# Turning the token rows of an expert block: two of three blocks by VectorE after a load in shares, the rest by TensorE

## The chip, the cores and the metric

The kernel runs on one core of a Trainium2 chip. The metric is the device time of one launch in microseconds (us); the profile is of one execution on the same core. All data are float32.

## What is computed

The input is 8 batches of 512 tokens with 256 features. Four layers follow one another, each with a layer norm ahead of it and a residual sum behind it: a state-space scan, a mixture of experts, causal attention with 16 heads, and the same mixture of experts once more. The change is in the mixtures of experts:

```python
x = hidden_states.reshape(-1, D)                    # 4096 tokens, D = 256
topk_idx, tw = _route(x, router_w, bias)            # 4 of 16 experts each
combine = (one_hot(topk_idx, E) * tw[..., None]).sum(1)
h = jnp.einsum('td,edf->etf', x, gate_w)            # F = 256
u = jnp.einsum('td,edf->etf', x, up_w)
y = jnp.einsum('etf,efd->etd', silu(h) * u, down_w)
routed = jnp.einsum('etd,te->td', y, combine)
sh = silu(x @ sh_gate_w) * (x @ sh_up_w) @ sh_down_w
return routed + sh
```

## The kernel before

The program runs in four stretches: the scan together with the first routing and the shared experts; the first routed stage; attention together with the second routing and shared experts; the second routed stage. Only the routed stages and what feeds them are touched.

**Sorted rows.** While a batch is routed, GpSimd scatters each token's row, once per chosen expert, into a DRAM buffer `xg[i]` that is sorted by expert. A row has 272 numbers: 256 normed features, 4 gains, 4 expert numbers and 8 copies of the token's number. A routed stage then goes through `xg[i]` in blocks of 128 rows, each of one expert; 136 blocks (`LIKELY`, L43) are always run.

**One block**, in `routed` (L823):

- `load` (L850): SyncE issues one DMA of 128 rows of 1088 B (L860) into a buffer `rows`. From block 2 on these come from a ring of nine (`KB`, L57), so the load of block n waits until the accumulation of block n - 9 has read its buffer.
- `fetch` (L863): ScalarE copies the expert's gate weights, VectorE its up weights, out of `w_all`, which holds all experts, into tiles with fixed addresses (L875). The place in `w_all` is a register value; `values` (L830) reads such values for four blocks at a time, the weights' places for TensorE, ScalarE and VectorE and the rows' places for SyncE.
- `turn` (L878): TensorE transposes the two halves of 128 features with the identity (`pt`, L882), and ScalarE copies the result back beside the rows (L883).
- `up` (L885): 8 matmuls, which the profile shows as 16 (L893), give gate and up products in one PSUM tile `ph` of a pool of four; ScalarE takes the sigmoid of the gate half (L901), VectorE multiplies twice (L902, L903) and works out each row's gain (L906, L914).
- `down` (L917): 2 matmuls, shown as 4 (L921); ScalarE scales the rows by their gain (L929); GpSimd adds them with an indirect DMA to the tokens' rows of a DRAM sum, `parts[i][n % 2]` (L930), so that even and odd blocks have a sum each.

**Order.** `run` (L940) writes the order out by hand: load n + 2, fetch n + 1, up n, turn n + 1, down n - 2. Engines run on their own and in order, so SyncE's loads run ahead as far as buffers come free. A scheduler may move an instruction within its engine's order unless it is pinned. Beside the blocks, at set block numbers, GpSimd's queue also carries other DMAs: in the first routed stage those that fetch a finished batch for attention (`prepared`, L1212, after block 64 and at the end), in the second those that fetch and store the sums of five finished batches (`early`, L1443, from blocks 64, 76, 88, 110 and 127). After the last accumulation the remaining batches are summed and stored.

PSUM pools of a routed stage are made by `banks_of(big=4, misc=2, y=2)` (L1412, L1420).

Of the kernel before, what the change touches and what calls it, by code (L numbers as in the profile page):

```python
# [11 lines left out]
AF = mybir.ActivationFunctionType  # L12
ALU = mybir.AluOpType
AX = mybir.AxisListType

P = 128
SQ = 32
QUAD = P // SQ
B, T, D = 8, 512, 256
NT = T // P  # L20
KD = D // P
# [37 lines left out]
PACE = 2  # L59
SENT = 4  # L60
HELD = 6


SUMMED = {0: DONE[0], 1: 76, 2: 88, 3: 110, 4: 127}
# [12 lines left out]
def tile_hybrid_block(  # L77
# [31 lines left out]
    def bank(shape, name: str, kind: str = "one"):  # L109
        kind = instead.get(kind, kind)  # L110
        return stage[kind].tile(shape, FP, tag=kind, name=name)

    def banks_of(**many):
        pools = ExitStack()
        for kind, bufs in many.items():
            stage[kind] = pools.enter_context(
                tc.tile_pool(name=f"ps_{kind}", bufs=bufs, space=bass.MemoryType.PSUM)
            )
        return pools
# [96 lines left out]
    def load_expert(e: int):  # L216
        at = e * WEXP
        gu = w_all[:, at : at + 2 * KD * F].rearrange("p (s k f) -> p s k f", k=KD, s=2)
        nc.sync.dma_start(out=gu[:, 0], in_=gate_w[e].rearrange("(k p) f -> p k f", p=P))
        nc.sync.dma_start(out=gu[:, 1], in_=up_w[e].rearrange("(k p) f -> p k f", p=P))  # L220
        nc.sync.dma_start(
            out=w_all[:, at + 2 * KD * F : at + WEXP].rearrange("p (k d) -> p k d", k=KF),
            in_=down_w[e].rearrange("(k p) d -> p k d", p=P),
        )
# [244 lines left out]
    class Scan:  # L469
# [7 lines left out]
        def load(self, b: int):  # L477
            if b + 1 < B and b > 0:
                with tc.issue_after(load_x(b + 1).ins):
                    for load in later[b - 1 :: shares]:  # L480
                        load()
# [341 lines left out]
    def routed(i: int, table, beside):  # L823

        weight_at, row_at, expert, many, _ = table
        ACT, DVE = mybir.EngineType.Activation, mybir.EngineType.DVE
        PE, SP = mybir.EngineType.PE, mybir.EngineType.SP
        held = {}

        def values(n: int):  # L830

            many = min(4, (LIKELY if n < LIKELY else NBLK) - n)
            _, w = nc.values_load_multi_w_load_instructions(
                weight_at[:, n : n + many],
                engines=[PE, ACT, DVE],
                min_val=0,
                max_val=(E - 1) * WEXP,
                skip_runtime_bounds_check_because="a count of at most E - 1 experts, times WEXP",
            )
            _, r = nc.values_load_multi_w_load_instructions(  # L840
                row_at[:, n : n + many],
                engines=[SP],
                min_val=0,
                max_val=NROW - BLK,
                skip_runtime_bounds_check_because="the blocks table stays within the sorted rows",
            )
            for j in range(many):
                held[n + j] = [w[j], r[j]]

        def load(n: int):  # L850
            if n not in held:
                values(n)
            if n < 2:


                rows = work.tile([P, NT, ROW], FP, tag="rows", name=f"rows_{i}_{n}")
                rows = rows.rearrange("p t c -> p (t c)")[:, 0 : 4 * D]
            else:
                rows = work.tile([P, 4 * D], FP, tag="kb4", name=f"rows_{i}_{n}", bufs=KB)
            nc.sync.dma_start(out=rows[:, 0:ROW], in_=xg[i][bass.ds(held[n][1], BLK), :])  # L860
            held[n].append(rows)

        def fetch(n: int):  # L863


            if n == 0:

                both = xpool.tile([P, NT, D], FP, tag="x", name=f"both_{i}").rearrange("p t d -> p (t d)")
            for half, (copy, name) in enumerate(((nc.scalar.copy, "gate"), (nc.vector.tensor_copy, "up"))):
                if n == 0:  # L870
                    here = both[:, half * KD * F : (half + 1) * KD * F]
                    copy = nc.vector.tensor_copy
                else:
                    here = work.tile([P, KD * F], FP, tag="col", name=f"{name}_{i}_{n}", bufs=COLS)
                copy(here, w_all[:, bass.ds(held[n][0] + half * KD * F, KD * F)])  # L875
                held[n].append(here)

        def turn(n: int):  # L878
            rows = held[n][2]
            pt = bank([P, KD, P], f"pt_{i}_{n}", "misc")  # L880
            for k in range(KD):
                nc.tensor.transpose(pt[:, k, :], rows[:, k * P : (k + 1) * P], ident)  # L882
            nc.scalar.copy(rows[:, ROW : ROW + D], pt.rearrange("p k q -> p (k q)"))  # L883

        def up(n: int):  # L885
            _, _, rows, *both = held[n]


            ph = bank([P, 2, KF * P], f"ph_{i}_{n}", "big")
            for s in range(2):  # L890
                for f in range(KF):
                    for k in range(KD):
                        nc.tensor.matmul(  # L893
                            ph[:, s, f * P : (f + 1) * P],
                            lhsT=both[s][:, k * F + f * P : k * F + (f + 1) * P],
                            rhs=rows[:, ROW + k * P : ROW + (k + 1) * P],
                            start=(k == 0),
                            stop=(k == KD - 1),
                        )
            act = rows[:, ROW + D : ROW + D + F]  # L900
            nc.scalar.activation(act, ph[:, 0, :], AF.Sigmoid)  # L901
            nc.vector.tensor_mul(act, ph[:, 0, :], act)  # L902
            nc.vector.tensor_mul(act, ph[:, 1, :], act)  # L903

            gain = small.tile([P, TK + 1], FP, tag="gain", name=f"gain_{i}_{n}", bufs=4)
            nc.vector.scalar_tensor_tensor(  # L906
                gain[:, 0:TK],
                rows[:, D + TK : D + 2 * TK],
                expert[:, n : n + 1],
                rows[:, D : D + TK],  # L910
                ALU.is_equal,
                ALU.mult,
            )
            nc.vector.tensor_reduce(gain[:, TK : TK + 1], gain[:, 0:TK], AX.X, ALU.add)  # L914
            held[n][3:] = [act, gain]

        def down(n: int):  # L917
            w, _, rows, act, gain = held.pop(n)
            py = bank([P, D], f"pyr_{i}_{n}", "y")
            for f in range(KF):  # L920
                nc.tensor.matmul(  # L921
                    py,
                    lhsT=act[:, f * P : (f + 1) * P],
                    rhs=w_all[:, bass.ds(w + 2 * KD * F + f * D, D)],
                    start=(f == 0),
                    stop=(f == KF - 1),
                )

            nc.scalar.mul(rows[:, 0:D], py, gain[:, TK : TK + 1])  # L929
            nc.gpsimd.indirect_dma_start(  # L930
                out=parts[i][n % 2],
                out_offset=bass.IndirectOffsetOnAxis(
                    ap=rows[:, D + 2 * TK : D + 2 * TK + 1].bitcast(U32), axis=0
                ),
                in_=rows[:, 0:D],
                in_offset=None,
                compute_op=ALU.add,
            )

        def run(first: int, last: int):  # L940
            load(first)
            load(first + 1)
            fetch(first)
            turn(first)
            for n in range(first, last + 2):
                if n + 2 < last:
                    load(n + 2)
                if n + 1 < last:
                    fetch(n + 1)
                if n < last:  # L950
                    up(n)
                if n + 1 < last:
                    turn(n + 1)
                if n - 2 >= first:
                    down(n - 2)
                    for work_beside in beside.get(n - 1, ()):
                        work_beside()


        _, (needed,) = nc.values_load_multi_w_load_instructions(  # L960
            many, min_val=0, max_val=NBLK, skip_runtime_bounds_check_because="a count of blocks"
        )
        with tc.If(needed > LIKELY):
            run(LIKELY, NBLK)
        run(0, LIKELY)
# [443 lines left out]
        table = stretch(Scan())  # L1409
        wqkv_sb, wo_sb = load_attention_weights()  # L1410

    with banks_of(big=4, misc=2, y=2):  # L1412
        instead["one"] = "misc"
        routed(0, table, {**prepared(0), **prepared(1)})
        del instead["one"]
# [1 line left out]
    with banks_of(one=4, pair=2):  # L1417
        table = stretch(Attention())

    with banks_of(big=4, misc=2, y=2):  # L1420

        beside = (nc.gpsimd, nc.gpsimd)

# [123 lines left out]
```

## Time and profile before

| what | before |
|---|---|
| median of 4 runs, lowest to highest | 1727.91 us, 1725.86 to 1729.31 |
| the profiled execution's own time, and its span | 1728.91 us, 1727.2 us |
| mean granted TensorE clock | 0.982 |
| busy: TensorE, its weight loads, VectorE | 95%, 70%, 66% of the span |
| busy: ScalarE, GpSimd | 44%, 45% |
| first routed stage: first load to last accumulation | 339.8 to 752.2 us |
| second routed stage: first load to last accumulation | 1281.1 to 1708.2 us |
| load of rows (SyncE), issue to landing | 2.6 us median, 272 of them |
| accumulation (GpSimd), issue to landing | 4.0 us median, 272 of them |

Busy shares are means over stretches of different kinds, so they have to be read stretch by stretch. Matmuls are pipelined: the time that one takes from the next is seen from start to start, not in its length. A "releaser" behind an arrow is the one whose event came last before an engine went on, as the profile infers it.

### The profile page before, as it was taken

What the parts mean: (1) busy time and instruction counts of PE and PEld (TensorE: products, weight loads), DVE (VectorE), ACT (ScalarE), POOL (GpSimd) and SP (SyncE); (2) the same over time, 40 slices, a digit from 0 to 9 for tenths busy, and PEclk for the clock granted to TensorE, in tenths of its full rate; (3) what the DMA queues carried; (4) which work ended last, traced back from release to release, by engine and by line L of the source; (5) the groups of instructions that cost most, each with busy time, mean ns of one, the idle gap of its engine ahead of it and who ended that gap; (6) DMA issues with size and microseconds to landing.
All of it is one profiled execution on the core that took longest, in us unless ns stands there. A gap on an engine that the chain in (4) does not pass through costs nothing. (4 is left out here: it accounts for less than half of the span.)

```text
span 1727.2 us, 32460 instructions
## 1 busy us (share of the span) xinstructions
PE 1634.7 (95%) x10448; PEld 1207.9 (70%) x10448; DVE 1131.9 (66%) x3503; ACT 767.6 (44%) x1684; POOL 771.4 (45%) x675
## 2 busy tenths in 40 slices
PE   6899998999999999999999999999999999999992
PEld 3566655589999999954445445444459999998992
DVE  7888877545555655567886687777735755555552
ACT  3223232155555555555444444444225555555551
POOL 3355555535555655530042242233434555555553
PEclk9999999999999999999999999999999999999996
DMA  5454333445555656531012211122544656666666
GB/s 161 138 183 157 135 107 114 161 90 96 96 97 106 108 96 96 101 74 38 25 65 69 70 62 60 64 83 85 178 142 83 96 95 97 114 132 125 115 123 165
DMA packets 149277, 181.36 MB, mean 105 GB/s; under 512 B 16144, under 2 KB 135984, under 8 KB 149104
## 3 DMA queue, kind: packets, MB, share of 16 engines
q0 software_dynamic: 54720, 82.57, 25.9%
q1 hardware_dynamic: 92576, 92.71, 18.0%
q10 hardware_dynamic: 1808, 3.93, 0.6%
q8 instruction: 88, 1.44, 0.3%
q14 instruction: 85, 0.70, 0.1%
HBM read 81.62 MB, written 97.53 MB: 104 GB/s over the span
## 5 line engine op out<-in xcount | busy, mean ns | idle before, releaser
L930 POOL DMA_INDIRECT part<-rows x272 | 425.2, 1563 | 345.5 <-ACT rows L929 241.7
L723 POOL DMA_INDIRECT xg<-sorted_m,slots_m x256 | 259.3, 1013 | 319.9 <-ACT slots_m L720 81.8
L893 PEld LDWEIGHTS ph<-rows,gate 128*128 128x128 f32 x2160 | 282.6, 192 | 15.6 <-ACT rows L883 1.6
L893 PE MATMUL ph<-rows,gate 128*128 128x128 f32 x2160 | 286.0, 276 | 0.6 <-ACT rows L883 0.6
L893 PE MATMUL ph<-rows,up 128*128 128x128 f32 x2160 | 285.9, 276 | 0.0
L921 PE MATMUL pyr<-w_all,rows 128*128 x1088 | 280.0, 380 | 0.4 <-DVE rstd_l L431 0.4
L893 PEld LDWEIGHTS ph<-rows,up 128*128 128x128 f32 x2160 | 263.5, 193 | 0.0
L901 ACT ACTIVATE rows<-ph 128x256 f32<-128x256 f32 x272 | 104.2, 383 | 330.0 <-PE ph L893 330.0
L902 DVE TENSOR_TENSOR rows<-ph,rows 128x256 f32<-128x256 f32 x272 | 115.2, 424 | 190.0 <-ACT rows L901 189.1
L921 PEld LDWEIGHTS pyr<-w_all,rows 128*128 128x128 f32 x1088 | 185.8, 191 | 14.7 <-ACT rows L929 0.8
L875 ACT COPY gate<-w_all 128x512 f32 x270 | 168.7, 626 | 14.3 <-PE ph L893 2.4
L1131 ACT ACTIVATE w_all<-ps_a 128x1024 f32<-128x1024 f32 x128 | 124.4, 1020 | 52.3 <-PE ps_a L1120 49.6
L875 DVE COPY up<-w_all 128x512 f32 x270 | 118.3, 438 | 31.3 <-PE ph L893 18.7
L929 ACT ACTIVATE rows<-pyr,gain 128x256 f32<-128x256 f32 x272 | 128.4, 472 | 14.3 <-PE pyr L921 13.2
L906 DVE SCALAR_TENSOR_TENSOR gain<-rows,expert_b 128x4 f32<-128x4 f32 x272 | 61.1, 225 | 111.0 <-ACT rows L929 82.1
L1120 PE MATMUL ps_a<-w_all 32*128 32x384 f32 (+3 forms) x1024 | 122.2, 475 | 7.7 <-ACT w_all L1131 6.7
L982 PE MATMUL pg_m<-xT_m,su_sb 128*128 128x512 f32 x256 | 125.5, 612 | 0.0
L982 PE MATMUL pg_m<-xT_m,sg_sb 128*128 128x512 f32 x256 | 122.4, 600 | 0.0
L1011 PE MATMUL pd_m<-sd_sb,act_m 128*128 128x256 f32 x512 | 121.2, 383 | 0.3 <-DVE act_m L998 0.2
L903 DVE TENSOR_TENSOR rows<-ph,rows 128x256 f32<-128x256 f32 x272 | 115.0, 424 | 8.4
L1011 PEld LDWEIGHTS pd_m<-sd_sb,act_m 128*128 128x128 f32 x512 | 95.9, 190 | 23.9 <-issue 6.7
L882 PE MATMUL pt<-ident,rows 128*128 128x128 f32 x544 | 103.9, 273 | 9.1 <-DMA rows<-xg 7.5
(223 smaller groups left out, 2134.6 us busy)
## 6 DMA issues: line engine op xcount, KB each, us to landing
rows<-xg SPq DMA_DIRECT2D x272, 136.0 KB, 2.6
part<-x SPq DMA_DIRECT2D x16, 512.0 KB, 3.4
part<-ys_m SPq DMA_DIRECT2D x14, 512.0 KB, 3.1
w_all<-in_L_ffn_gate_w_dram SPq DMA_DIRECT2D x24, 256.0 KB, 5.1
w_all<-in_L_ffn_up_w_dram SPq DMA_DIRECT2D x24, 256.0 KB, 5.3
w_all<-in_L_ffn_down_w_dram SPq DMA_DIRECT2D x24, 256.0 KB, 5.4
sum<-part POOLq DMA_DIRECT2D x10, 512.0 KB, 4.2
xg<-zeros SPq DMA_DIRECT2D x34, 136.0 KB, 2.7
```

Of the source, the lines that this page charges most:

```text
L723: nc.gpsimd.indirect_dma_start(out=xg[i], out_offset=bass.IndirectOffsetOnAxis(ap=slots[:, at : at + 1], axis=0), in_=rows[:, t, :], in_of ...
L875: copy(here, w_all[:, bass.ds(held[n][0] + half * KD * F, KD * F)])
L893: nc.tensor.matmul(ph[:, s, f * P : (f + 1) * P], lhsT=both[s][:, k * F + f * P : k * F + (f + 1) * P], rhs=rows[:, ROW + k * P : ROW + (k ...
L902: nc.vector.tensor_mul(act, ph[:, 0, :], act)
L903: nc.vector.tensor_mul(act, ph[:, 1, :], act)
L921: nc.tensor.matmul(py, lhsT=act[:, f * P : (f + 1) * P], rhs=w_all[:, bass.ds(w + 2 * KD * F + f * D, D)], start=(f == 0), stop=(f == KF - 1),
L929: nc.scalar.mul(rows[:, 0:D], py, gain[:, TK : TK + 1])
L930: nc.gpsimd.indirect_dma_start(out=parts[i][n % 2], out_offset=bass.IndirectOffsetOnAxis(ap=rows[:, D + 2 * TK : D + 2 * TK + 1].bitcast(U ...
L982: made = nc.tensor.matmul(dst, lhsT=w[:, k, f * P : (f + 1) * P], rhs=xnT[:, k, :], start=(k == 0), stop=(k == KD - 1),)
L1011: nc.tensor.matmul(py[:, j, :], lhsT=acts[n][:, f, t * P : (t + 1) * P], rhs=shared[n][3][:, f, :], start=(n == 0 and f == 0), stop=(n == ...
L1120: nc.tensor.matmul(ps[j // 2][:, j % 2, col : col + n], lhsT=k_sb[w][r, o, c * P : (c + 1) * P], rhs=q_sb[r, o, c * P : T], start=True, st ...
L1131: nc.scalar.activation(es[two], ps[two][:, :, 0:cols], AF.Exp, scale=ATT_SCALE)
```

## The change

The loads of rows and weights stay on SyncE, which issued them before. What differs:

- Experts' gate and up weights are loaded so that partition p holds features 2p and 2p + 1, and not p and 128 + p.
- `heads` are the first two blocks of a stage and every third block. They are loaded as before and turned by TensorE, which now takes every second feature from the rows.
- Any other block is loaded by five DMAs: four shares of 64 features, each into 32 partitions with pieces of 256 B (32 x 4 x 64), and one with the last 16 numbers of all rows. One VectorE transpose of 32x32 squares (128x256) then makes of it what `turn` made.
- SyncE's register values are read apart from the others', eight at a time (`places`); loads are written four blocks ahead (`AHEAD`).
- Gate and up products have a PSUM tile each, from pools of two and two.
- The first multiply of block n is pinned behind the turn of block n + 1, and the gain behind the second multiply.

```diff
@@ load_expert
-        nc.sync.dma_start(out=gu[:, 0], in_=gate_w[e].rearrange("(k p) f -> p k f", p=P))
-        nc.sync.dma_start(out=gu[:, 1], in_=up_w[e].rearrange("(k p) f -> p k f", p=P))
+        nc.sync.dma_start(out=gu[:, 0], in_=gate_w[e].rearrange("(p k) f -> p k f", p=P))
+        nc.sync.dma_start(out=gu[:, 1], in_=up_w[e].rearrange("(p k) f -> p k f", p=P))
@@ load
-            nc.sync.dma_start(out=rows[:, 0:ROW], in_=xg[i][bass.ds(held[n][1], BLK), :])
+            block = bass.ds(held[n][-1], BLK)
+            if n in heads:
+                nc.sync.dma_start(out=rows[:, 0:ROW], in_=xg[i][block, :])
+            else:
+                for a in range(QUAD):
+                    nc.sync.dma_start(
+                        out=rows[a * SQ : (a + 1) * SQ, 0:D].rearrange("s (b c) -> s b c", b=QUAD),
+                        in_=xg[i][block, a * KD * SQ : (a + 1) * KD * SQ].rearrange("(b s) c -> s b c", s=SQ),
+                    )
+                nc.sync.dma_start(out=rows[:, D:ROW], in_=xg[i][block, D:ROW])
@@ turn
-            for k in range(KD):
-                nc.tensor.transpose(pt[:, k, :], rows[:, k * P : (k + 1) * P], ident)
-            nc.scalar.copy(rows[:, ROW : ROW + D], pt.rearrange("p k q -> p (k q)"))
+            xT = rows[:, ROW : ROW + D]
+            if n in heads:
+                pt = bank([P, KD, P], f"pt_{i}_{n}", "misc")
+                for k in range(KD):
+                    nc.tensor.transpose(pt[:, k, :], rows[:, 0:D].rearrange("p (q k) -> p k q", k=KD)[:, k], ident)
+                nc.scalar.copy(xT, pt.rearrange("p k q -> p (k q)"))
+            else:
+                turns[n] = nc.vector.transpose(
+                    xT.rearrange("p (k b s) -> p k b s", k=KD, b=QUAD),
+                    rows[:, 0:D].rearrange("p (b i k) -> p k b i", b=QUAD, k=KD),
+                )
@@ up
-            ph = bank([P, 2, KF * P], f"ph_{i}_{n}", "big")
+            ph = [bank([P, KF * P], f"ph_{i}_{n}_{s}", f"big{s}") for s in range(2)]
...
+            with tc.issue_after(turns.pop(n + 1).ins) if n + 1 in turns else nullcontext():
+                nc.vector.tensor_mul(act, ph[0], act)
+            made = nc.vector.tensor_mul(act, ph[1], act)
@@ run
+            heads.update((first, first + 1, *range(first, last, BY_PE)))
...
+                load_to(n + AHEAD)
+                if n + 2 < last and n + 2 not in known:
+                    values(n + 2)
...
-                if n + 1 < last:
+                if n + 1 in heads and n + 1 < last:
                     turn(n + 1)
+                if n + 2 not in heads and n + 2 < last:
+                    turn(n + 2)
@@ the pools of both routed stages
-    with banks_of(big=4, misc=2, y=2):
+    with banks_of(big0=2, big1=2, misc=2, y=2):
```

## The prediction

> **What bounds the kernel now.** The busy table by stretch comes first (columns: window and length; busy us with counts of TensorE, its weight loads, VectorE, ScalarE, GpSimd; granted clock; DMA share; GB/s). 440:540 lies in the first routed stage (348 to 741 us), 1483:1695 in the second half of the second one (1293 to 1708 us).
>
> ```profile
> 440.00:540.00 100.00, 100.00 (x770) 96.37 (x770) 56.55 (x175) 54.80 (x140) 54.34 (x35) 1.00 0.60 96
> 1483.00:1695.00 212.00, 204.39 (x1553) 195.32 (x1552) 119.76 (x353) 111.91 (x280) 115.11 (x82) 1.00 0.64 121
> 1695.00:1727.00 32.00, 0.91 (x5) 0.45 (x3) 3.65 (x3) 0.95 (x2) 10.34 (x8) 0.56 0.70 194
> ```
>
> In the first row TensorE never rests and every other engine is near 55%. The second row has 7.6 us of rest, and in the third TensorE is done while 32 us still pass. So there are two regimes. For the first, TensorE's timeline (start, length, operation):
>
> ```profile
> 527.84 0.38 PE L882 MATMUL pt<-ident,rows 128*128 128x128 f32 x2
> 528.06 1.03 PE L921 MATMUL pyr<-w_all,rows 128*128 x4
> 528.93 1.05 PE L893 MATMUL ph<-rows,gate 128*128 128x128 f32 x8
> 529.82 1.06 PE L893 MATMUL ph<-rows,up 128*128 128x128 f32 x8
> 530.71 0.38 PE L882 MATMUL pt<-ident,rows 128*128 128x128 f32 x2
> ```
>
> Starts matter here, since ends overlap: a block takes 530.71 - 527.84 = 2.87 us, and its two transposes 528.06 - 527.84 = 0.22 (0.21 at other places; I use 0.215), not the 0.55 that two durations of 273 ns suggest. For the second regime, GpSimd's timeline:
>
> ```profile
> 1597.65 1.55 POOL L930 DMA_INDIRECT part<-rows  x1 [1.25 <-ACT gate L875]
> 1599.51 1.55 POOL L930 DMA_INDIRECT part<-rows  x1 [0.30 <-issue]
> 1602.86 1.55 POOL L930 DMA_INDIRECT part<-rows  x1 [1.80 <-ACT rows L883]
> 1604.71 1.55 POOL L930 DMA_INDIRECT part<-rows  x1 [0.30 <-issue]
> 1607.65 1.55 POOL L930 DMA_INDIRECT part<-rows  x1 [1.39 <-ACT rows L929]
> ```
>
> An accumulation into a part waits for the last one into the same part. Two of them take 1607.65 - 1597.65 over two pairs, so 5.0 us a pair, **2.5 us a block**. The ScalarE releasers named are not the cause: block 107's down starts at 1616.56 and its accumulation only at 1619.45, 0.30 us after the one before. From block 63 on, where the sums of finished batches begin to hold GpSimd up (about 7.5 us each of the five), an accumulation never goes out as soon as its rows are ready (1.8 us after its down, as in the steady part). At the end the gap is 13 us: the last down starts at 1694.9, the last accumulation at 1708.22. The chain of waits agrees:
>
> ```profile
> 1708.22 3.75 DMA part<-rows
> 1713.39 8.41 DMA sum<-part
> ```
>
> So the last 72 blocks of the second stage end with GpSimd's chain, and only the other 136 + 64 = 200 blocks are TensorE's.
>
> **The change, part by part.** *Transposes moved.* By the diff, heads (blocks 0, 1 and every third) are 47 of 136, so 89 blocks per stage are turned by VectorE: 41 of the first 64 and 48 of the last 72. TensorE saves 89 x 0.215 = 19.1 us in the first stage, 41 x 0.215 = 8.8 in the first part of the second, and 48 x 0.215 = 10.3 in the rest, which I cost at nothing, since GpSimd's chain ends it. ScalarE loses a copy of 367 ns in those blocks; it waits for TensorE anyway.
>
> *VectorE's turn.* Its nearest rows:
>
> ```profile
> L606 DVE STREAM_TRANSPOSE logit_m<-pl_m 128x128 f32<-128x128 f32 x16 | 5.0, 310 | 17.6 <-PE pl_m L595 17.5
> L1178 DVE STREAM_TRANSPOSE oT_a<-tr_a 128x512 f32<-128x512 f32 x16 | 11.2, 698 | 0.3
> ```
>
> Linear between 310 and 698, 128x256 is 0.44 us. VectorE goes from 56% of 2.87 to (1.62 + 0.67 x 0.44) / 2.73 = 70%: hidden by TensorE. But it is in order: by the built program's order most turns of block m stand ahead of the multiplies of block m - 3, late in each stage about one in six ahead of m - 4. Behind them queue the multiplies, the gains and the weight copy; TensorE waits for those.
>
> *Loads in shares.* A load now:
>
> ```profile
> L860 SPq DMA_DIRECT2D rows<-xg x272: 332/333/762, 339.8 to 1684.7; - x136
> DMA to landing us min/median/max: 2.0/2.6/4.2
> ```
>
> Loads that wait for nothing follow each other every 0.55 us (354.5, 355.0, 355.6). Five instead of one make SyncE 11 x 0.55 = 6.1 us in each three blocks of 8.2: hidden. The fourth share lands 3 x 0.55 + 2.6 = 4.25 us after the first is issued, and the turn is done at about 4.9, with its waits. Today a load is issued 11.9 us before its block's first matmul (block 60: 511.1 against 523.19), the time at which its buffer comes free, nine blocks back; with faster blocks some 11.1. A turn ahead of m - 3 needs 4.9 + 0.42 (a multiply) + 2.73 = 8.05, since with two PSUM gate tiles instead of four whole ones that multiply must free the tile for block m - 1. One ahead of m - 4 needs 10.8. Both just fit.
>
> They don't fit after GpSimd's stall at block 63 of the first stage: load 73 is issued at 555.6, 4.9 us before its matmuls at 560.48, and less the 1.4 that faster blocks use up, 3.5 against 8.05; load 82 would have 4.6 against 10.8. TensorE then stands about 5 to 6 us, where it stood 0.9 before: **+5 us** (0 to +8). The same happens four times in the second stage's end, where it uses up GpSimd's backlog: 0 (-10.3 if the chain gives way, +8 if not).
>
> *DMA cost.* A block's load was 8 packets per engine, 63 ns each in the records (0.5 us). Now it is 32 of 256 B and 8 of 64 B. The records have 13 ns at 176 B, 27 at 512 and 46 at 1024; I take 18 and 11, 0.66 us. From above, every packet at the present mean of 63 ns gives 2.5 us: the engines would then carry 1.22 (accumulations, 0.60 x 2.87 less 0.5) + (2 x 2.5 + 0.5) / 3 = 3.05 us a block, above 2.73; that end gives 200 x 0.18 + 72 x 0.55 = +76, 1805, the far end of the slower rival. Below, the price is no gain, since 0.5 us is what fewer and longer packets take. My value is the one that the 176 and 512 rows enclose.
>
> The Trainium skill, "DMA: Bandwidth & Descriptors", Specifications, speaks against this part: below 512 B the engine reads, modifies and writes, so that such packets miss line rate. No row here shows a 256 B packet. If one costs what 512 B do, the block's load is, by estimate, 0.95 us instead of 0.66, and my sum stays.
>
> Each accumulation now also waits for four more semaphores (17 to 27 ns each at SyncE): 0.05 us a block where the chain binds, 72 x 0.05 = **+4**.
>
> *The rest.* The heads' transposes read rows with a step of two: 0, or at most a weight load twice as long, 142 ns x 188 = +26, if the step halves its rate; no row has such a step, and I take the plain one. Gate tiles of their own let the sigmoid start a half earlier; its result is used two blocks later: 0. Register loads split between SyncE and the rest, experts' rows in another order (2 KB runs): as many bytes in stages that wait for neither: 0.
>
> **Sum.** -19.1 + 5 - 8.8 + 0 + 4 = -19. The profiled execution took 1728.91 us (span 1727.2), 1.0 above the median 1727.91: 1728.9 - 19 = **1710**, with 1702 to 1720 as this case's own range.
>
> **Rivals.** *All of it comes through.* If loads are early enough and GpSimd's chain moves with TensorE, 38.2 us: 1691. For it: the steady leads fit. Against it: the 13 us at the end.
>
> *A longer chain, a wash.* If the shares' packets delay accumulations by 0.5 us, GpSimd's pair takes 5.5 and its block 2.75, just TensorE's new pace: -26 for the first 200 blocks, +6 of stalls, 72 x 0.25 = +18: 1727.
>
> *Slower.* The same chain, from 0.5 us of delay on. At 0.7 it runs at 2.84 a block everywhere: 200 x -0.03 = -6, 72 x 0.35 = +25, +5 of stalls: 1752. For it: accumulations already spread from about 1 us to 2 where a load runs beside them (512 to 514 us in the records), and shares run nearly all the time. Against it: the bytes are the same, and short packets hold up a waiting one for less time.
>
> **Chances.** My case 0.50, all of it 0.14, the wash 0.11, slower 0.25. What can be told from no change is 0.2%, 3.4 us. Faster: 0.50 + 0.14 + 0.04 of the wash = 0.68; same 0.06; slower 0.26. The range leaves out half of the first rival (0.07) and the upper half of the last (0.12): 1692 to 1752.
>
> **What would show it.** Right: blocks without pt take 2.66 us and heads 2.87, the mean in the first stage's steady part is 2.73; turns near 0.44 us; accumulations still 2.5 us apart and the last one some 10 us after the last down; a pause of about 5 us near block 73. Wrong: 256 B packets of 40 ns or more, accumulations landing over 4.5 us after issue, TensorE waiting for VectorE's multiplies or for turns in the steady part, heads' weight loads near 280 ns.

## The result and the profile after

The changed kernel took **1732.12 us** (median of 52 runs, 1724.98 to 1738.63), the kernel before 1728.93 in the same comparison (78 runs): ratio 1.0017, 95% interval 1.001 to 1.0025. So it is slower by about 3 us; the forecast was 1710. The profiled execution took 1731.75 us (span 1730.0).

The busy table by stretch of the changed kernel, for the stretches that the prediction read (columns as there: TensorE, its weight loads, VectorE, ScalarE, GpSimd, granted clock, DMA share, GB/s; the ends are moved with the last up at 1697):

```profile
440.00:540.00 100.00, 99.54 (x741) 93.11 (x740) 63.02 (x205) 55.85 (x120) 55.91 (x36) 1.00 0.68 100
1483.00:1698.00 215.00, 199.62 (x1425) 186.04 (x1424) 121.61 (x392) 106.40 (x228) 112.86 (x81) 0.96 0.67 119
1698.00:1730.00 32.00, 3.58 (x21) 2.87 (x20) 5.90 (x8) 1.80 (x4) 10.30 (x8) 0.63 0.71 194
```

The first row is as forecast: TensorE works nearly all the time on fewer instructions. In the second it rests 15.4 of 215 us, where it rested 7.6 of 212, and its granted clock is 0.96, where it was 1.00. Cutting the two profiled executions at the same events (an "up" counts from its first matmul) shows where the time went:

| stretch (us) | before | after | moved | forecast |
|---|---|---|---|---|
| start to first up | 350.8 | 351.5 | +0.7 | 0 |
| first stage, first to last up | 388.4 | 382.0 | -6.4 | -14 |
| last up to the second stage's first up | 554.1 | 564.9 | **+10.8** | 0 |
| second stage, first up to block 63's | 182.4 | 175.0 | -7.4 | -8.8 |
| block 63's up to the last accumulation | 232.5 | 237.1 | +4.6 | +4 |
| last accumulation to the end | 18.9 | 19.5 | +0.6 | 0 |

Three things are to be seen in the trace. **The heads.** TensorE's timeline of the changed kernel (start, length, operation), one head with its neighbours:

```profile
431.09 1.05 PE L920 MATMUL ph<-rows,gate 128*128 128x128 f32 x8
...
432.88 0.40 PE L903 MATMUL pt<-ident,rows 128*128 128x128 f32 x2
...
434.06 1.16 PE L920 MATMUL ph<-rows,gate 128*128 128x128 f32 x8
...
436.82 1.05 PE L920 MATMUL ph<-rows,gate 128*128 128x128 f32 x8
...
439.47 1.06 PE L920 MATMUL ph<-rows,gate 128*128 128x128 f32 x8
```

A period is the time from one up to the next. The one with the transposes is 434.06 - 431.09 = 2.97 us, the head's own 436.82 - 434.06 = 2.76, and the third 439.47 - 436.82 = 2.65. Only this last was forecast (2.87, 2.66, 2.66). ScalarE's timeline says why:

```profile
433.12 0.62 ACT L894 COPY gate<-w_all 128x512 f32 x1 [0.55 <-PE ph L920]
433.65 0.36 ACT L904 COPY rows<-pt 128x256 f32<-128x256 f32 x1
```

L904, without which the head's up can't start, stands behind the gate weights' copy for the block two later, which nobody needs yet. Of the 43 triples of such periods in the first stage, 27 take 8.37 or 8.38 us and ten 8.18 or 8.19; before, 8.60 or 8.61 was usual.

**Turns that stand too early.** The page's row of VectorE's turns, and VectorE's timeline after GpSimd's stall in the first stage:

```profile
L907 DVE STREAM_TRANSPOSE rows<-rows 128x256 f32<-128x256 f32 x178 | 79.0, 444 | 170.7 <-DMA rows<-xg 168.7
```

```profile
553.87 0.45 DVE L907 STREAM_TRANSPOSE rows<-rows 128x256 f32<-128x256 f32 x1 [7.91 <-DMA rows<-xg]
554.24 0.38 DVE L894 COPY up<-w_all 128x512 f32 x1
554.54 0.41 DVE L930 TENSOR_TENSOR rows<-ph,rows 128x256 f32<-128x256 f32 x1
```

The turn takes 444 ns as forecast, but VectorE stood 168.7 us before turns for their loads. In the place shown it stands 7.91 us, and a weight copy and multiplies of earlier blocks, whose inputs may long be there, stand behind it. Here are TensorE's waits for VectorE's multiplies in the two routed stages (us in total, times, longest), the first stage's and the second's:

```profile
PE ph L920 <- DVE rows L930: 4.3, 3, 3.6
```

```profile
PE ph L920 <- DVE rows L930: 14.4, 7, 3.9
```

Before, TensorE waited in the first stage for ScalarE alone, and in neither stage for VectorE's multiplies:

```profile
PE ph L893 <- ACT rows L883: 2.4, 2, 2.1
```

These rests cost clock too. The changed kernel's clock in two places, each just behind a rest of 3.6 and 3.9 us:

```profile
556.00:559.50 3.50, 3.50 (x16) 3.14 (x15) 2.98 (x11) 1.00 (x2) 2.56 (x2) 0.51 0.91 129
1580.20:1583.40 3.20, 3.20 (x13) 2.84 (x12) 2.02 (x7) 0.93 (x2) 2.08 (x2) 0.50 0.80 130
```

Of TensorE's 12 rests of over 0.2 us in the two stages, the five longest, 1.87 to 3.87 us, each have such a stretch that begins in them or within 2 us behind them, and the others have none. In the kernel before, whose longest rest there is 2.19 us, there is none, nor in e9 below behind one of 2.84 us.

**The end of the first stage.** TensorE's and GpSimd's timelines behind the last up (733.5; before 739.2), each followed by that of the kernel before:

```profile
744.77 1.89 PE L1124 MATMUL pv_a<-w_att,xT_l 128*128 128x256 f32 x8
751.67 3.78 PE L1124 MATMUL pv_a<-w_att,xT_l 128*128 128x256 f32 x8 [5.01 <-ACT v_a L1131]
```

```profile
751.06 3.62 PE L1083 MATMUL pv_a<-w_att,xT_l 128*128 128x256 f32 x16
```

```profile
748.60 1.55 POOL L959 DMA_INDIRECT part<-rows  x1 [1.21 <-issue]
749.58 1.64 POOL L1101 MEMSET v_a<- 128x1148 f32 x1
```

```profile
749.30 1.54 POOL L930 DMA_INDIRECT part<-rows  x1 [0.56 <-issue]
750.28 1.63 POOL L1060 MEMSET v_a<- 128x1148 f32 x1
752.22 1.55 POOL L930 DMA_INDIRECT part<-rows  x1 [0.31 <-ACT w_all L1075]
```

TensorE comes to the attention's product with v earlier than before (744.77, not 751.06), but GpSimd's memset of v's tile comes hardly earlier (749.58, not 750.28). One reason is its place: before, the stage's last accumulation stood behind it, and in the changed kernel it stands behind that one too, which costs 748.60 - 745.85 = 2.75 us. ScalarE's copy of the product's first half must wait for the memset. TensorE rests 5.0 us, from 746.66 to 751.67, and the granted clock, 1.00 in both of these windows before, falls:

```profile
749.00:759.00 10.00, 7.33 (x26) 5.18 (x27) 0.69 (x1) 2.51 (x6) 3.27 (x3) 0.66 0.55 171
759.00:769.00 10.00, 7.97 (x38) 2.35 (x36) 4.92 (x12) 7.03 (x9) 0.00 (x0) 0.83 0.00 0
```

Two views for the second regime. GpSimd's timeline, in the window that the prediction showed, and the end of the chain of waits:

```profile
1599.52 1.54 POOL L959 DMA_INDIRECT part<-rows  x1 [2.66 <-ACT rows L958]
1601.94 1.54 POOL L959 DMA_INDIRECT part<-rows  x1 [0.89 <-ACT rows L958]
1604.59 1.54 POOL L959 DMA_INDIRECT part<-rows  x1 [1.11 <-ACT rows L958]
```

```profile
1710.47 3.90 DMA part<-rows
```

In this window GpSimd has caught up: its accumulations go out 1.8 to 2.0 us after their downs, and TensorE is what is late. Where GpSimd has a backlog, a pair of accumulations takes some 4.7 us in the median (some 5.0 before). The last accumulation follows the last up (1697.0) by 13.5 us, before by 16.8.

### The profile page after: what moved, and what is told of

The parts are those of the page before. It is cut to its first block, busy times and chain, and to the rows that moved or that the text cites. A ratio compares the mean times of both kernels' runs of the same rounds, so it can differ in the third digit from the quotient of the medians.

```text
span 1730.0 us, 34472 instructions
## 1 busy us (share of the span) xinstructions
PE 1623.4 (94%) x10092; PEld 1177.7 (68%) x10092; DVE 1157.9 (67%) x3681; ACT 757.0 (44%) x1506; POOL 771.8 (45%) x675
## 4 chain that ended last, share of the span: by engine, by line
PE 27%; DMA 16%; DVE 5%; issue 3%; SPq 1%; POOL 1%; ACT 0%; ACTq 0%; POOLq 0%; DVEq 0%
DMA part<-rows 14%; PE ps_a L1161 5%; PE ph L920 4%; PE po_a L1196 3%; PE pg_m L1023 3%; PE pq_a L1106 3%; PE pd_m L1052 2%; PE pyr L950 2%; PE py_a L459 2%; PE pv_a L1124 2%; DMA rows<-xg 1%; SPq L875 1%; POOL xg L725 1%; DVE w_all L1175 1%; DVE w_all L1183 1%
## 5 line engine op out<-in xcount | busy, mean ns | idle before, releaser
L920 PE MATMUL ph<-rows,gate 128*128 128x128 f32 x2160 | 294.0, 280 | 18.8 <-DVE rows L930 18.8
L920 PE MATMUL ph<-rows,up 128*128 128x128 f32 x2160 | 289.4, 278 | 1.0 <-DVE rows L931 1.0
L950 PEld LDWEIGHTS pyr<-w_all,rows 128*128 128x128 f32 x1088 | 189.9, 194 | 14.9
L907 DVE STREAM_TRANSPOSE rows<-rows 128x256 f32<-128x256 f32 x178 | 79.0, 444 | 170.7 <-DMA rows<-xg 168.7
L1052 PEld LDWEIGHTS pd_m<-sd_sb,act_m 128*128 128x128 f32 x512 | 95.9, 190 | 23.9 <-issue 6.7
L1161 PEld LDWEIGHTS ps_a<-w_all 32*128 32x128 f32 x1024 | 49.0, 189 | 71.2 <-ACT w_all L1172 27.4
```

Source lines behind the costliest of these rows:

```text
L920: nc.tensor.matmul(ph[s][:, f * P : (f + 1) * P], lhsT=both[s][:, k * F + f * P : k * F + (f + 1) * P], rhs=rows[:, ROW + k * P : ROW + (k ...
L950: nc.tensor.matmul(py, lhsT=act[:, f * P : (f + 1) * P], rhs=w_all[:, bass.ds(w + 2 * KD * F + f * D, D)], start=(f == 0), stop=(f == KF - 1),
L1052: nc.tensor.matmul(py[:, j, :], lhsT=acts[n][:, f, t * P : (t + 1) * P], rhs=shared[n][3][:, f, :], start=(n == 0 and f == 0), stop=(n == ...
L1161: nc.tensor.matmul(ps[j // 2][:, j % 2, col : col + n], lhsT=k_sb[w][r, o, c * P : (c + 1) * P], rhs=q_sb[r, o, c * P : T], start=True, st ...
```

## Experiments

Two theories stood against each other. *The author's:* TensorE's freed time is real, and three places in other engines' orders give it back: turns too early in VectorE's order, the heads' copy behind a weight copy in ScalarE's, the memset behind the accumulations in GpSimd's. *Rivals:* the freed time was never worth anything, since GpSimd's chain sets the end; or the loads in shares cost it through the DMA engines. Each kernel was timed beside the kernel before on the same chip, but not all on one chip, so they are compared by their ratios; "against before" is 1728 us times (ratio - 1), uncertain by as much as the interval says. e1, e5, e8 and e9 leave out part of the computation or do it on features in the wrong order, so that they are of use for their times alone.

| kernel | median us | ratio, 95% interval | against before, us |
|---|---|---|---|
| changed kernel | 1732.12 | 1.0017 (1.001 to 1.0025) | +2.9 |
| e1: before, rows copied and not turned | 1991.76 | 1.1534 (1.1506 to 1.1562) | +265 |
| e2: before, memset on VectorE | 1724.97 | 1.0001 (0.9983 to 1.0019) | +0.2 |
| e3: changed, memset on VectorE | 1720.51 | 0.9974 (0.996 to 0.9988) | -4.5 |
| e4: changed, turns later | 1712.78 | 0.9922 (0.9899 to 0.9945) | -13.5 |
| e5: before, 89 blocks a stage not turned | 1698.61 | 0.9844 (0.9824 to 0.9865) | -27.0 |
| e6: changed, turns later, memset | 1708.56 | 0.9897 (0.9876 to 0.9917) | -17.8 |
| e7: as e6, and the head's copy first | 1700.28 | 0.9847 (0.9825 to 0.987) | -26.4 |
| e8: as e6, one load a block | 1707.35 | 0.9892 (0.9872 to 0.9912) | -18.7 |
| e9: before, only the tail not turned | 1725.36 | 0.9991 (0.9973 to 1.001) | -1.6 |
| e10: as e7, all by VectorE | 1766.30 | 1.0234 (1.0202 to 1.0265) | +40 |
| e11: as e7, whole PSUM tiles | 1703.37 | 0.9881 (0.985 to 0.9911) | -20.6 |
| e12: changed, the head's copy first | 1716.93 | 0.9951 (0.9934 to 0.9968) | -8.5 |

**e1 and e5: is TensorE's time worth having?** e1 put a plain ScalarE copy in the place of the transposes:

```diff
+            if n > 1 and n % 3:
+                nc.scalar.copy(rows[:, ROW : ROW + D], rows[:, 0:D])
+                return
```

> The kernel before, but in the 89 blocks of a stage that the change gives to VectorE the rows are not turned at all: ScalarE copies them as they are (that part of the computation is left out). One load, no shares, no VectorE turn. Theory (TensorE's time is worth having, but part of it is given back at places that GpSimd's accumulations end): first stage some 17 to 19 us shorter on TensorE, then a pause ahead of attention of 2 to 6 us with a clock below 1; second stage some 9 us shorter up to block 63 and nothing behind it; in all 15 to 25 us faster than before. Rival (GpSimd's chain or something else ends the stages anyway, TensorE's transposes are covered): within 5 us of before.

Measured: 1991.76 us. No expectation holds, for a reason that has its use. The first stage's ups alone took 518 us, and these are its longest waits in total in that stretch (us in total, times, longest):

```profile
ACT rows L881 <- DMA rows<-xg: 217.4, 75, 8.8
```

The copies stand early in ScalarE's order and wait there for their loads, with its sigmoids and weight copies queued behind them: the fault suspected of VectorE, made far larger in another engine. The run says nothing of TensorE's time. e5 leaves the step out altogether:

```diff
+            if n > 1 and n % 3:
+                return
...
+            at = 0 if n > 1 and n % 3 else ROW
...
-                            rhs=rows[:, ROW + k * P : ROW + (k + 1) * P],
+                            rhs=rows[:, at + k * P : at + (k + 1) * P],
```

> This is the kernel before, with the 89 blocks of each stage that are not heads left without any turn: their multiplies take the rows as loaded. It leaves out part of the computation (those blocks' transposes, 2 matmuls and a ScalarE copy each) and adds nothing to it. My theory: TensorE's time is worth its whole length in the first stage (89 x 0.215 = 19 us) and in the first part of the second (41 x 0.215 = 9 us), so 15 to 28 us below the kernel before, and the changed kernel loses it elsewhere. Theory that GpSimd's accumulations set the end of both stages, so that TensorE's time is worth next to nothing: within 5 us of the kernel before.

Measured: -27.0 us (-30.4 to -23.3). The periods are 2.87, 2.65, 2.65, the first stage's ups take 369.7 us (before 388.4). That TensorE's time is worth nothing is refuted; the gross saving agrees with what the prediction summed, 19.1 + 8.8 = 27.9.

**e9: and in the second stage's tail?** The same edit, for the second stage's blocks from 64 on alone.

> The kernel before, with 48 blocks of the second stage's last 72 (the same ones that the change gives to VectorE) left without any turn, and nothing else touched. It leaves out those blocks' transposes and copies. The prediction put nothing on TensorE's time there, since GpSimd's chain of accumulations was to set the end: within 3 us of the kernel before. Theory that GpSimd only shifts TensorE's stalls, and that the chain has room to follow: 48 x 0.215 = 10 us below it, as the kernel without turns suggests (29.5 us in all, of which 28 are explained without the tail; so at least 2 and up to 10).

Measured: -1.6 us (-4.7 to +1.7). Nothing that can be told from no change, though TensorE had 10.3 us less to do. That the whole 10.3 us comes through is refuted; a gain of up to some 5 us is not. Where the rest goes is only in part seen. Count as a *stall* what a period of over 3.1 us takes beyond 2.97, the longest undisturbed one: the second stage's stalls are 14.4 us in e9's profile and 11.8 in that of the kernel before, but 6.2 in that of e2 below, whose stages are the same code as before, so that single executions differ by more than this. The prediction's second regime stands by the time, not by these profiles.

**e2 and e3: the memset.** In either kernel:

```diff
-                nc.gpsimd.memset(v_sb, 1.0)
+                nc.vector.memset(v_sb, 1.0)
```

> The kernel before, with attention's memset of v on VectorE instead of GpSimd. Control for the next run. Both theories: within 2 us of before, since TensorE does not wait for that memset there.

> The changed kernel, with attention's memset of v on VectorE. Theory (the memset waits behind the first stage's last accumulations, TensorE stands 5 us for it and then runs some 3 us at a lower clock): 7 to 9 us faster than the changed kernel, some 5 us faster than before; no pause at pv and a clock of 1.0 there. Rival (the pause only takes the place of another wait for the same accumulations, a little later in attention): less than 3 us gained.

Measured: +0.2 us on the kernel before; on the changed one -4.5 against before, so -7.4 against the changed kernel (uncertain by some 3). TensorE's timeline of e3:

```profile
744.79 3.62 PE L1124 MATMUL pv_a<-w_att,xT_l 128*128 128x256 f32 x16
```

The product comes at the same time, but in one piece, with no wait; from the first stage's last up to the second's first up are 554.5 us, as before the change (554.1). So one instruction in the wrong queue made that row long. How much it made of the +10.8 is less sure: the row takes 564.9 and 565.3 us in the changed kernel and e12, where TensorE meets the memset late, but from 553.5 to 559.1 in the ten profiles where it doesn't (e1 and e4 apart), and 557.7 in e9, whose code is that of the kernel before up to there. The timing, 7.4, is the better measure.

**e4: turns later.** The turn of block m is pinned behind the second multiply of block m - 2:

```diff
+                last = mades.get(n - 2)
+                with tc.issue_after(last.ins) if last is not None else nullcontext():
                     turns[n] = nc.vector.transpose(
...
-            made = nc.vector.tensor_mul(act, ph[1], act)
+            made = mades[n] = nc.vector.tensor_mul(act, ph[1], act)
```

> The changed kernel, with VectorE's turn of block m pinned behind the second multiply of block m - 2, so that no multiply of an earlier block queues behind a turn that waits for its load. Theory (turns that stand too early in VectorE's order make TensorE stand after GpSimd's stalls): TensorE's pauses of over 0.2 us fall from 9 to about 3 us in the first stage and from 26 to about 15 in the second; 6 to 11 us faster than the changed kernel. Rival (the loads in shares themselves come too late, wherever the turn stands): pauses stay, within 3 us of the changed kernel.

Measured: -13.5 against before, -16.4 against the changed kernel: more than expected. VectorE's timeline of e4 at the same stall, and TensorE's waits for VectorE in the second stage:

```profile
550.21 0.21 DVE L938 SCALAR_TENSOR_TENSOR gain<-rows,expert_b 128x4 f32<-128x4 f32 x1
552.98 0.47 DVE L910 STREAM_TRANSPOSE rows<-rows 128x256 f32<-128x256 f32 x1 [2.56 <-DMA rows<-xg]
```

```profile
PE ph L923 <- DVE gain L946: 7.1, 7, 2.9
```

That wait is now 2.56 and not 7.91 us, and the multiplies go ahead of it. The first stage's ups take 376.0 us (382.0 in the changed kernel), its stalls 1.9 (8.3; before 3.0); block 63's up to the last accumulation 226.6 (237.1). Behind block 63 of the second stage TensorE rests less, 7.6 us against 15.4, and its clock is higher. The rows of the two kernels, the changed one first:

```profile
1473.00:1698.00 225.00, 209.62 (x1499) 195.41 (x1499) 128.45 (x414) 112.14 (x241) 117.53 (x84) 0.96 0.68 118
```

```profile
1463.00:1675.00 212.00, 204.45 (x1490) 190.38 (x1489) 126.56 (x412) 111.62 (x239) 117.02 (x83) 0.98 0.69 124
```

At 0.96 some 9 of 225 us of clock are missing, at 0.98 some 4 of 212. So by estimate up to 5 of the 10.5 us gained here are the clock's, and the early turns cost more than the rests themselves.

**e6 and e7: the mends together.** e6 has both edits; e7 adds this:

```diff
-                copy(here, w_all[:, bass.ds(held[n][0] + half * KD * F, KD * F)])
+                first = turned_back.get(n - 2) if name == "gate" else None
+                with tc.issue_after(first.ins) if first is not None else nullcontext():
+                    copy(here, w_all[:, bass.ds(held[n][0] + half * KD * F, KD * F)])
...
-                nc.scalar.copy(xT, pt.rearrange("p k q -> p (k q)"))
+                turned_back[n] = nc.scalar.copy(xT, pt.rearrange("p k q -> p (k q)"))
```

> The changed kernel with both mends: turns pinned behind the second multiply of block m - 2 (13 us below the kernel before by itself) and the attention's memset moved from GpSimd to VectorE (5 below it by itself). If the two losses are separate places, the rest at the attention's first product with v in the late-turn kernel (3.3 us) goes, and the time between the first stage's last up and the second's first falls from 560.1 to about 554.5: 17 to 19 us below the kernel before. Rival: the late turns already took most of what the memset costs, since GpSimd then has less to catch up: no more than 14 below.

> The kernel with both mends, and the head's own copy out of PSUM put ahead of ScalarE's gate copy of the block two later. My theory: the gate copy ahead of it makes two of every three heads' triples 0.19 us longer; with the order turned round the periods are 2.88, 2.65, 2.65 everywhere, 5 us less in the first stage and up to 4 in the second: 5 to 9 us below the kernel with both mends. Rival: the weights' copy is then what comes late for its own block, or the head costs TensorE 0.3 us by its strided transposes whatever ScalarE does: within 2 us of it.

Measured: e6 -17.8, as expected, though the row from last to first up is 557.4 and not 554.5: the wait is gone, but the clock granted in 749 to 759 us is 0.83. e7 is 8.6 below e6, near the upper end of the 5 to 9 that was expected. ScalarE's timeline of e7:

```profile
433.86 0.37 ACT L907 COPY rows<-pt 128x256 f32<-128x256 f32 x1 [0.79 <-PE pt L906]
434.39 0.62 ACT L897 COPY gate<-w_all 128x512 f32 x1 [0.16 <-ACT rows L907]
```

With the two copies turned round the periods are 2.88, 2.65, 2.65, and the first stage's ups take 371.0 us. That the heads' strided transposes cost 0.3 us is refuted: a head's period is 2.88 or 2.89 where a plain one's was 2.87. **e7 is the fastest kernel here that computes the whole result**: 26.4 us (22.5 to 30.2) below the kernel before, 29.3 below the changed one, and as fast as e5, which saves the same transposes and pays nothing for it (ratios 0.9847 and 0.9844). So what e7 keeps of the change beside the mends (loads in shares, register reads apart, weights in another order, the other pins, PSUM tiles) costs nothing together that can be told within some 5 us.

**e12: the head's copy alone.** The third edit on the changed kernel.

> The changed kernel with one mend alone: the head's own copy ahead of ScalarE's gate copy of the block two later; turns early and memset on GpSimd as the change has them. My theory: periods 2.88, 2.65, 2.65 in the steady part, 4 to 5 us less per stage there, but part of it given back since faster blocks leave a late load's turn even less time: 3 to 9 us below the changed kernel, which is from nothing to 6 us below the kernel before. Rival: without the late turns it brings nothing at all, since the stalls grow by as much: within 2 us of the changed kernel.

Measured: -8.5 against before, -11.4 against the changed kernel; the expected 3 to 9 lies within the error of that difference (some 3 us). The stalls stayed (8.4 us in the first stage, 23.9 in the second; 8.3 and 24.2 in the changed kernel). So there is no sign that the early turns gave any of it back.

**e8: the price of the shares.** In e6 every block is loaded by one DMA:

```diff
-            if n in heads:
+            if True:
```

> The kernel with both mends, but every block's rows loaded by one DMA in plain order, as before the change, and turned by VectorE all the same. What it leaves out: the features of the 89 blocks then stand in another order than the weights', so its products are other ones; the amount of work is the same. My theory: the shares' packets (18 ns each, about as many bytes) and SyncE's issues are hidden, and a load lands 1.6 us earlier, which helps only where loads are late: 0 to 4 us below the kernel with both mends. Rival: shares in short packets hold up accumulations and the weights, and the price of the change lies there: 8 us or more below it.

Measured: 0.9 below e6, with an error of some 5. No price of the shares can be told here, though they are dearer to the DMA engines: the row of the loads' queue in 440 to 540 us (packets, MB, share of 16 engines) has 18.3% in the kernel before, 18.2% in e8 and in the changed kernel

```profile
q1 hardware_dynamic: 18481, 4.92, 26.0%
```

**e10: why not all blocks?** In e7, BY_PE = 1000, so that only a stage's first two blocks are heads.

> The kernel with all three mends, and all blocks but the first two of a stage loaded in shares and turned by VectorE. TensorE is free of 90 more transposes of 0.215 us. Theory that TensorE sets the pace and VectorE (63% busy now, some 72% then) has room: 2.65 us a block everywhere, 10 us less in the first stage and 3 to 10 in the second, so 10 to 17 us below the kernel with three mends. Rival: with no head between them every block waits for a turn just made, and SyncE's five issues a block delay the loads after each of GpSimd's stalls: no faster than it, or up to 10 us slower.

Measured: +40 against before, some 66 above e7. Both theories missed it: the rival named the right queue, but allowed 10 us. SyncE's queue in the steady part of e10, and what TensorE does then:

```profile
499.98 1.84 SPq L876 DMA_DIRECT2D rows<-xg  x4
502.01 0.36 SPq L880 DMA_DIRECT2D rows<-xg  x1
502.62 1.88 SPq L876 DMA_DIRECT2D rows<-xg  x4
```

```profile
504.82 1.13 PE L925 MATMUL ph<-rows,gate 128*128 128x128 f32 x8 [0.19 <-DVE rows L912]
```

Undisturbed, five issues take 502.62 - 499.98 = 2.64 us, all that a block has; with its register reads SyncE comes to 2.98 us a block (160 issues, 0.596 apart, in 440 to 540 us; it waits only 2.3 of these 100 us for other engines). So the loads have no lead: from block 6 of the first stage to block 74, a block's first share goes out 4.2 to 5.6 us before its up, where a load of the kernel before had some 12. VectorE waits for them and TensorE for VectorE, 3.09 us a block. The theory had counted VectorE's time, not SyncE's. With heads the same count is 11 x 0.53 = 5.8 us in 8.2.

**e11: PSUM tiles of their own.**

```diff
-            ph = [bank([P, KF * P], f"ph_{i}_{n}_{s}", f"big{s}") for s in range(2)]
+            whole = bank([P, 2, KF * P], f"ph_{i}_{n}", "big")
+            ph = [whole[:, s, :] for s in range(2)]
...
-    with banks_of(big0=2, big1=2, misc=2, y=2):
+    with banks_of(big=4, misc=2, y=2):
```

> The kernel with all three mends, but with gate and up results in one PSUM tile of two halves again, four of them, as before the change, and not in two pools of two tiles each. The prediction put nothing on this part. My theory: the results are used two blocks later and neither form is waited for, so within 2 us of the kernel with three mends. Rival: tiles of their own let sigmoid and multiplies free PSUM a half earlier, and without them the late turns hold TensorE up: 4 us or more above it.

Inconclusive between theory and rival: -20.6 against before, e7 -26.4, with intervals that overlap, from two chips. In the profiles they are alike: 2.725 and 2.730 us a block in the first stage's blocks 10 to 60.

## Why the prediction was wrong

The gains were right and the losses were not. The prediction saw that engines work in order, and asked this of VectorE alone, and there for too little. By its own steps:

- **Transposes moved, -27.9: right.** e5 has -27.0, e9 nothing for the last 72 blocks.
- **"Both just fit", and the pauses, +5 and 0: the size was wrong.** The pause near block 73 was right: stalls in the first stage went from 3.0 to 8.3 us. But undoing the early turns brought 16.4 us (e4). The two profiled executions differ by 20.5: 6.0 in the first stage, 4.8 at its end and 10.5 behind block 63 of the second, less small differences the other way. Behind block 63 of the second stage the prediction took 0 of "-10.3 if the chain gives way, +8 if not", on the ground that pauses only use up GpSimd's backlog. They went past it: GpSimd is seen without a backlog at 1600 us. Nor did the sum have a term for the clock, which was granted at half behind the longer rests (above). The table's +4.6 for this stretch is flattered: 232.5 us in the profiled execution of before is long, as e2, whose stages are the same code, has 223.1 there.
- **"ScalarE loses a copy; it waits for TensorE anyway": wrong.** The sum was of ScalarE's time, and its order was not looked at. The heads' periods cost 0.19 us in two triples of three; turning two copies round gave 8.6 us (e7 against e6) and 11.4 (e12 against the changed kernel).
- **The first stage's end, not priced at all: wrong.** The prediction let the first stage end with TensorE's last up, and saw GpSimd's 13 us of delay only in the second. The stage after it needs GpSimd too; a memset that TensorE had not met late now held it for 5.0 us: +10.8 in the profile, 7.4 by timing (e3). TensorE's lead alone does not do it. In e5 TensorE is further ahead (the product at 733.76), but the memset (733.34) keeps its place ahead of the last accumulation, and nothing waits. The changed kernel has it behind the last accumulation, by an order that the prediction did not look at.
- **Extra semaphores, +4: wrong, small.** A pair of accumulations in the backlog takes some 4.7 us, not more than the 5.0 of before; why it takes less is not shown.
- **DMA cost: right.** 256 B packets take 18 ns in the median and 22.2 in the mean, 64 B ones 11.7. By the means a block's load is 32 x 22.2 + 8 x 11.7 = 0.80 us (forecast 0.66, which is what the medians give); accumulations land 4.1 us after issue in 440 to 540 us (3.9 before). The "longer chain" and "slower" rivals, which needed 0.5 us more, did not happen. So it is luck that 1732 lies within 1692 to 1752: that end was put there for a chain slowed by DMA, and the slower result came by ways that no rival had.
- **For the page that spoke against it** (the Trainium skill, "DMA: Bandwidth & Descriptors", Specifications), the estimate of 0.95 us was made for its rule, at a 512 B packet's price; the measured 0.80 lies between the two, with more time a byte in 256 B packets (18 ns) than in 512 B ones (27), as the page's rule would have it. e8 shows no sign that either was on the path.
- **VectorE's turn 0.44 us, heads' strided transposes 0: right.** 444 ns; 0.02 us a head with the copy in order (e7), although their weight loads take 200 ns where plain ones took 142.
- **Two slips in the working change nothing.** Block 60's load is issued 523.19 - 511.1 = 12.1 us ahead, not 11.9, and the wash rival's 200 blocks at 2.75 us are -24 and not -26.

Added up from the runs: -27.0 for the transposes; the three mends together bring 29.3 (e7 against the changed kernel), by themselves 16.4, 7.4 and 11.4, which overlap by 5.9. -27.0 + 29.3 = +2.3, and the change measured +2.9: within the error of these differences, some 4 us each, nothing is left unexplained.

What stays open is the granted clock. In e7 TensorE is never held up at v, and yet is given 0.50 in 748 to 753 us, after three rests of 0.4 to 0.9 us that the kernel before has as well, at 1.00. Nor is this the mends' doing: e9, with the code of the kernel before up to there, has the same three rests and falls too. The rows of e7, the kernel before and e9:

```profile
748.00:753.00 5.00, 5.00 (x16) 1.22 (x18) 1.82 (x6) 1.84 (x3) 0.00 (x0) 0.50 0.00 0
```

```profile
759.00:769.00 10.00, 8.34 (x58) 3.16 (x59) 6.72 (x16) 7.02 (x10) 0.00 (x0) 1.00 0.32 107
```

```profile
764.00:769.00 5.00, 5.00 (x18) 1.19 (x18) 3.05 (x8) 2.51 (x4) 0.00 (x0) 0.66 0.13 43
```

So how much of the memset's 7.4 us and of the early turns' 16.4 is the clock's and how much the waits' own was not told apart. The Trainium skill, "TensorE: Matmul & The Clock Gate", Part 1, has TensorE at half its clock after an idle window of about 3.4 us, with windows that run freely, so that the same rests may be caught in one run and not in another. The 0.50 of e7 is such a half, and the difference between two runs fits; that rests of less than a microsecond can do it, the page does not say.

## What to carry to other kernels

Freeing the engine that sets the pace is worth what the sum says only if each other engine's order lets it run ahead: list, for every in-order queue, what stands ahead of the instruction that the fast engine needs next, and whether that is waiting for something later (a turn that waits for a load, a weight copy that nobody needs yet, a memset behind accumulations). An engine with 40% of idle time can be late all the same, and an instruction that waits for a DMA belongs as late in its queue as its user allows. Follow the gain past the end of its stage, to the first thing there that another engine prepares, and when a DMA is split, count the issues of its queue (2.64 us for five here) against the pace.

## What the runs showed of the hardware

- In the changed kernel the granted TensorE clock was 0.66 in 749 to 759 us, around the end of a rest of 5.0 us, and 0.50 or 0.51 for some 3 us behind rests of 3.6 and 3.9 us in the routed stages. It was 0.50 in 748 to 753 us of e7 after rests of less than a microsecond; in the kernel before, the same short rests at 759 to 763 us left it at 1.00.
- DMA issues on one queue that wait for nothing followed each other every 0.51 us in e10 (median of 160 in 440 to 540 us), the last of five to the next block's first 0.61; a packet of 256 B took a median of 18 ns in the changed kernel, and each DMA engine has eight of them to a share.
- Transposes on TensorE that read every second element had weight loads of 200 ns (median) instead of 142, and yet a head's period was only 0.02 us longer.
